# Expert weights in 2 KB rows and quarter-row gathers turned by VectorE, in a one-core transformer block with routed experts

## The chip, the core and the metric

The kernel runs on one core of a Trainium2 chip. A core has a matrix engine (TensorE, called PE in the profile, with its weight loads listed as PEld), a vector engine (VectorE, DVE), a scalar engine (ScalarE, ACT), a general engine (GpSimd, POOL) and a queue engine that only issues transfers (SyncE, SP). All work on a common on-chip memory of 128 partitions, SBUF; TensorE writes its results to a second memory, PSUM. The metric is the time of one execution on the device in microseconds.

## The reference

The block is attention followed by a mixture of experts, on 2048 tokens of 512 features in float32. Only the second half matters here:

```python
h = _layernorm(x) * (1 + cb) + sb
logits = flat @ Wr + router_bias
topk_scores, topk_idx = jax.lax.top_k(softmax(logits), K)      # K = 4 of E = 64 experts
xb = zeros((E, CAP, D)).at[eid, pos].set(flat[tok], mode='drop')   # CAP = 128 seats each
h = silu(einsum('ecd,edh->ech', xb, Wg)) * einsum('ecd,edh->ech', xb, Wu)
yb = einsum('ech,ehd->ecd', h, Wd)
out.at[tok].add(yb[eid, pos] * w)          # plus two shared experts applied to every token
```

Each expert gets up to 128 tokens. Its three matrices are Wg and Wu of 512 x 128 and Wd of 128 x 512.

## The kernel before, in words

Attention runs first, for about 1730 us. Then the output projection is made tile by tile (128 tokens each), normalised, stored to a DRAM array `h2d`, transposed into `h2T`, and routed: `choose`, `positions` and `seat_tokens` build a PSUM table that says which token sits on which seat of which expert. From it the last `seat_tokens` makes `tok` (128 seats x 64 experts of row numbers of `h2d`), lines 998 to 1002.

The expert stage is a software pipeline over 64 experts. For expert e:

- `load_up` (L1088, L1089) and `load_down` (L1094) bring its weights through SP's queue, three experts ahead. Feature k*128+p lies in partition p, block k, so every row of the transfer is 512 bytes.
- `load_xb` (L1323) lets POOL gather the expert's 128 token rows of 2 KB from `h2d` by `tok`, one indirect transfer per expert, three buffers deep.
- `expert_turn` (L1333, L1335) transposes the gathered tile on TensorE, four 128 x 128 blocks into the PSUM tile `tpx`, which ScalarE copies to `xbT`.
- `expert_up` (L1340) multiplies the four blocks of `xbT` by the weights into the PSUM tile `pse`, of which there is only one (`bufs=1`). ScalarE and VectorE make `he` of it (L1099 to L1101).
- `expert_mid` (L1355, L1357) transposes `he`, and `expert_down` (L1361, L1363) multiplies by Wd into `psy`, scales it to `y` and lets ACT's queue store it to `ybd`.

`expert_step(e)` puts four pieces in this order: the turn of expert e+1, with the gather of e+3 ahead of it; the up product of e; the middle of e-1; the down product of e-2. Each piece has a cost in columns: 512, 1024, 128 and 512.

A second stream, the shared experts, is merged with the first. Its units are products into the PSUM tiles `pst` (L1195, three buffers, read by VectorE at L1207 to L1235), and its down products are blocks of 16 matmul records, `psd` (L1257). `merge` takes the piece of whichever stream has done the smaller share of its total cost, and so fixes the program order on each engine. There is no other scheduler: each engine works through its own instructions in that order, and waits where a semaphore tells it to. After the stage a tail gathers the expert outputs from `ybd` and adds them up.

Just ahead of the stage lies the head, ten shared products (`LEAD`) with the last routing steps between them; the last `seat_tokens` comes after product 7, and `token_sum` and `weight_sum` follow on VectorE.

Of the kernel before, what the change touches and what calls it, by code (L numbers as in the profile page):

```python
# [18 lines left out]
P = 128  # L19
# [4 lines left out]
def adaln_block_kernel(  # L24
# [43 lines left out]
    ident = const.tile([P, P], F32)  # L68
# [11 lines left out]
    h2d = dram.tile([N, D], F32)  # L80
# [40 lines left out]
    with ExitStack() as att:  # L121
# [140 lines left out]
        with tc.tile_pool(name="pre", bufs=1) as pre, tc.manual_schedule():  # L262
# [401 lines left out]
        xts = {}  # L664
# [138 lines left out]
    keep = ctx.enter_context(tc.tile_pool(name="keep", bufs=1))  # L803
# [8 lines left out]
    psO = ctx.enter_context(tc.tile_pool(name="psO", bufs=2, space=PSUM))  # L812
# [5 lines left out]
    rt = rts.enter_context(tc.tile_pool(name="rt", bufs=1))  # L818
# [4 lines left out]
    iota = rt.tile([P, E], F32)  # L823
    places = rt.tile([P, CAP], F32)
    own = rt.tile([P, 1], F32)
    tok = keep.tile([CAP, E], U32)
    hs_ = {}
    mvs = {}
    logits = {}
# [5 lines left out]
    def route_consts():  # L835
        nc.sync.dma_start(out=wr, in_=Wr.rearrange("(k p) e -> p k e", p=P))
        nc.sync.dma_start(out=rb, in_=router_bias.partition_broadcast(P))
        make_upper_triangular(nc, before, val=1.0, diag=False)
        nc.gpsimd.memset(onesb, 1.0)
        nc.gpsimd.iota(  # L840
            iota, pattern=[[1, E]], base=0, channel_multiplier=0,
            allow_small_or_imprecise_dtypes=True,
        )
        nc.gpsimd.iota(
            places, pattern=[[1, CAP]], base=0, channel_multiplier=0,
            allow_small_or_imprecise_dtypes=True,
        )
        nc.gpsimd.iota(
            own, pattern=[[0, 1]], base=0, channel_multiplier=1,
            allow_small_or_imprecise_dtypes=True,  # L850
        )

    def load_x(j):
        nc.sync.dma_start(
            out=acc[:, 4 * j : 4 * j + 4, :],
            in_=x[0, j * 512 : (j + 1) * 512, :].rearrange("(i p) d -> p i d", p=P),
        )
# [125 lines left out]
    def seat_tokens(b):  # L983


        t0, nt = BLOCKS[b]
        seat, who = seats.pop(b)
        for n in range(nt * K):
            i, k = divmod(n, K)
            nc.tensor.matmul(  # L990
                out=table,
                lhsT=seat[:, n, :],
                rhs=who[:, i, k].rearrange("p j e -> p (j e)"),
                start=(b == 0 and n == 0),
                stop=(b == len(BLOCKS) - 1 and n == nt * K - 1),
            )
        if b == len(BLOCKS) - 1:
            tb = rt.tile([CAP, 2 * E], F32, name="tb")
            nc.vector.tensor_copy(tb, table)
            nc.vector.scalar_tensor_tensor(  # L1000
                tok, tb[:, E:], float(P), tb[:, :E], ALU.mult, ALU.add
            )

    table = psO.tile([CAP, 2 * E], F32, name="table", tag="tr")
    ALL = ((0, 4), (4, 8), (8, 12), (12, 16))
# [12 lines left out]
    with tc.manual_schedule():  # L1018
# [18 lines left out]
        for t in range(NE, NT):  # L1037
            pr, i = divmod(t, 2)
            if i == 0 and 3 <= pr < NP - 1:
                load_ab(pr + 1, heads=ALL)  # L1040
            if i == 1 and pr >= NP - 1 - S:
                s = pr - (NP - 1 - S)
# [31 lines left out]
    with ExitStack() as ex:  # L1074
# [9 lines left out]
        downs = {}  # L1084

        def load_up(e):
            w = ewp.tile([P, DC, 2, HE], F32, name="wgu")
            nc.sync.dma_start(out=w[:, :, 0, :], in_=Wg[e].rearrange("(k p) h -> p k h", p=P))  # L1088
            nc.sync.dma_start(out=w[:, :, 1, :], in_=Wu[e].rearrange("(k p) h -> p k h", p=P))  # L1089
            weights[e] = w  # L1090

        def load_down(e):
            downs[e] = ewp.tile([P, D], F32, name="wd")
            nc.sync.dma_start(out=downs[e], in_=Wd[e])  # L1094

        def glu(dst, pg, pu, width):

            sig = sgp.tile([P, width], F32, name=f"sig{width}")
            nc.scalar.activation(sig, pg, AF.Sigmoid)  # L1099
            nc.vector.tensor_mul(sig, sig, pg)  # L1100
            nc.vector.tensor_mul(dst, sig, pu)  # L1101
# [213 lines left out]
        xbp = wts.enter_context(tc.tile_pool(name="xbp", bufs=2))  # L1315
        xbs = {}
        xts = {}
        ups = {}
        hts = {}

        def load_xb(e):
            xbs[e] = xbp.tile([CAP, D], F32, name="xb", bufs=3)
            nc.gpsimd.indirect_dma_start(  # L1323
                out=xbs[e][:, :],
                out_offset=None,
                in_=h2d[:, :],
                in_offset=bass.IndirectOffsetOnAxis(ap=tok[:, e : e + 1], axis=0),
            )

        def expert_turn(e):  # L1330
            tp = psO.tile([P, DC, P], F32, name="tpx", tag="tr")
            for k in range(DC):
                nc.tensor.transpose(tp[:, k, :], xbs[e][:, k * P : (k + 1) * P], ident)  # L1333
            xts[e] = xbp.tile([P, DC, CAP], F32, name="xbT")
            nc.scalar.copy(xts[e], tp)  # L1335

        def expert_up(e):
            ps = psO.tile([P, 2 * HE], F32, name="pse", tag="pl", bufs=1)
            for k in range(DC):
                nc.tensor.matmul(  # L1340
                    out=ps,
                    lhsT=xts[e][:, k, :],
                    rhs=weights[e][:, k].rearrange("p i h -> p (i h)"),
                    start=(k == 0),
                    stop=(k == DC - 1),
                )
            if e + 3 < E:
                load_up(e + 3)
            he = xbp.tile([CAP, HE], F32, name="he")
            glu(he, ps[:, :HE], ps[:, HE:], HE)  # L1350
            ups[e] = he

        def expert_mid(e):
            tp = psO.tile([P, CAP], F32, name="tph", tag="tr")
            nc.tensor.transpose(tp, ups[e], ident)  # L1355
            hts[e] = xbp.tile([P, CAP], F32, name="heT")
            nc.scalar.copy(hts[e], tp)  # L1357

        def expert_down(e):
            ps = psO.tile([CAP, D], F32, name="psy", tag="y")  # L1360
            nc.tensor.matmul(out=ps, lhsT=hts[e], rhs=downs[e], start=True, stop=True)  # L1361
            y = xbp.tile([CAP, D], F32, name="y")
            nc.vector.tensor_mul(y, ps, gb)  # L1363
            nc.scalar.dma_start(out=ybd[e * CAP : (e + 1) * CAP, :], in_=y)

        def expert_step(e):
            out = []

            def turn():
                if e + 3 < E:  # L1370
                    load_xb(e + 3)
                expert_turn(e + 1)

            def down():
                expert_down(e - 2)
                if e + 1 < E:
                    load_down(e + 1)

            if e + 1 < E:
                out.append((512, turn))  # L1380
            if e < E:
                out.append((1024, lambda: expert_up(e)))
            if 0 <= e - 1 < E:
                out.append((128, lambda: expert_mid(e - 1)))
            if e >= 2:
                out.append((512, down))
            return out
# [20 lines left out]
                store(t)  # L1408

        with tc.manual_schedule():  # L1410
            for e in range(3):
                load_xb(e)
            expert_turn(0)
            for j in range(1, 5):
                weight_sum(0, j)
            experts = []
            for e in range(E + 2):
                experts += expert_step(e)
            merge([experts, shared[LEAD:-TAIL]], [])
        wts.close()  # L1420
        ygp = ex.enter_context(tc.tile_pool(name="ygp", bufs=4, side="right"))
        with tc.manual_schedule():
# [55 lines left out]
```

## Time and profile before

| What | us |
|---|---|
| Median of three runs (2456.49 to 2463.15) | 2459.82 |
| The profiled execution's own time | 2473.66 |
| Its span in the profile | 2471.9 |
| PE busy in the span | 2376.8 |
| DVE busy | 1512.2 |
| ACT busy | 838.1 |
| POOL busy | 224.1 |
| Expert stage, from the first up product to the last (1974 to 2335) | 361 |

The page names every group of instructions by line, engine and tile, for example `L1340 PE MATMUL pse<-wgu,xbT`: line 1340, TensorE, the result `pse` out of `wgu` and `xbT`. Behind it stand the shapes, the count, the busy time in us, the mean duration of one in ns, and the idle time ahead of it with what ended it. A float32 product shows as two records for each matmul of the program, a transpose as one. The ends of matmuls are modelled: the distance between the starts of two neighbours is what the engine takes for one. A timeline row gives a start and a duration in us.

### The profile page before, as it was taken

Reading aid. Unit: us, or ns where it says so; the run is one execution under the profiler, and the core shown is the slowest. Engines: PE = TensorE matmul, PEld = TensorE weight load, DVE = VectorE, ACT = ScalarE, POOL = GpSimd, SP = SyncE. Lnnn points to the kernel's source line nnn. Section 1 sums busy time; section 2 is a strip of 40 time slices with the busy share of each in tenths; the row PEclk is TensorE's granted clock in tenths of the full one; section 3 lists DMA queues with packets and bytes.
Section 4 is the critical chain, followed back from the end, with each engine's and each line's share of the span. In section 5 each row is a group of like instructions: output and inputs, shape, how many; then the busy total and the mean of one; then the engine's idle time right before and its main releaser. Section 6 shows DMA issues by size and latency. Waiting matters only on the chain. (4 is left out here: it accounts for less than half of the span.)

```text
span 2471.9 us, 26333 instructions
## 1 busy us (share of the span) xinstructions
PE 2376.8 (96%) x8406; PEld 1504.6 (61%) x8406; DVE 1512.2 (61%) x2878; ACT 838.1 (34%) x1785; POOL 224.1 (9%) x286
## 2 busy tenths in 40 slices
PE   7999999999999999999999999998999999999989
PEld 3656656566565665666656656555444476877734
DVE  5367666676666766667667676663655563644654
ACT  3244443443444434444344444432111222222200
POOL 0000000000000000000000000000000011111163
PEclk9999999999999999999999999999999999999989
DMA  4234444454354443444445444564432378778564
GB/s 137 62 79 113 116 118 106 97 135 107 94 133 104 101 119 91 111 111 104 116 96 122 105 103 118 161 174 128 152 119 85 102 206 249 230 212 252 171 190 133
DMA packets 223682, 325.23 MB, mean 132 GB/s; under 512 B 31876, under 2 KB 138424, under 8 KB 223544
## 3 DMA queue, kind: packets, MB, share of 16 engines
q1 hardware_dynamic: 196664, 252.21, 39.5%
q0 software_dynamic: 17664, 54.54, 7.3%
q10 hardware_dynamic: 9216, 16.78, 1.8%
q8 instruction: 68, 1.11, 0.2%
q14 instruction: 70, 0.57, 0.1%
HBM read 138.86 MB, written 41.94 MB: 73 GB/s over the span
## 5 line engine op out<-in xcount | busy, mean ns | idle before, releaser
L516 ACT ACTIVATE p<-ps,nm 128x1024 f32<-128x1024 f32 (+7 forms) x384 | 332.2, 865 | 897.0 <-DVE nm L514 411.5
L569 PE MATMUL po<-pt,v 128*128 128x256 f32 (+1 forms) x2304 | 575.5, 369 | 38.4 <-ACT at L578 33.4
L569 PEld LDWEIGHTS po<-pt,v 128*128 128x128 f32 x2304 | 426.5, 191 | 288.2 <-issue 190.5
L497 PE MATMUL ps<-kt,qt 128*128 128x512 f32 (+3 forms) x1280 | 531.2, 531 | 19.2 <-ACT p L516 16.8
L510 DVE TENSOR_REDUCE nm<-ps 128x1 f32<-128x1024 f32 (+7 forms) x384 | 348.8, 908 | 56.6 <-PE ps L497 47.8
L551 DVE STREAM_TRANSPOSE pt<-pt 128x1664 f32<-128x1664 f32 (+2 forms) x160 | 317.9, 1987 | 44.1 <-DMA pt<-p 40.5
L497 PEld LDWEIGHTS ps<-kt,qt 128*128 128x128 f32 x1280 | 234.7, 190 | 179.2 <-issue 137.0
L424 PE MATMUL pv<-wv,hT 128*128 128x256 f32 x1024 | 240.8, 379 | 2.2 <-ACT v L431 2.2
L581 POOL DMA_DIRECT2D atd<-at x128 | 80.1, 627 | 1649.4 <-ACT at L578 1111.7
L424 PEld LDWEIGHTS pv<-wv,hT 128*128 128x128 f32 x1024 | 194.4, 190 | 31.2 <-ACT v L431 3.0
L704 ACT ACTIVATE p<-p,rs 128x1024 f32<-128x1024 f32 (+7 forms) x256 | 200.0, 805 | 6.2 <-DVE rs L472 5.8
L509 DVE TENSOR_TENSOR ps<-ps,causal 128x128 f32<-128x128 f32 x256 | 74.1, 289 | 176.9 <-PE ps L497 174.5
L1048 PE MATMUL pso<-hT,T 128*128 128x512 f32 x384 | 175.6, 602 | 0.0
L217 PE MATMUL pqk<-T,sw 128*128 128x512 f32 x360 | 169.2, 592 | 0.0
L1340 PE MATMUL pse<-wgu,xbT 128*128 128x256 f32 x512 | 121.1, 379 | 0.0
L1048 PEld LDWEIGHTS pso<-hT,T 128*128 128x128 f32 x384 | 70.3, 193 | 72.1 <-issue 71.3
L217 PE MATMUL pqk<-hT,wq 128*128 128x512 f32 x240 | 113.7, 596 | 0.0
L1257 PE MATMUL psd<-wsd,hs 128*128 128x512 f32 x256 | 111.5, 592 | 0.0
L1340 PEld LDWEIGHTS pse<-wgu,xbT 128*128 128x128 f32 x512 | 93.8, 190 | 11.7 <-issue 1.0
L217 PEld LDWEIGHTS pqk<-T,sw 128*128 128x128 f32 x360 | 68.4, 190 | 47.7 <-issue 43.0
L1323 POOL DMA_INDIRECT xb<-h2d,tok x64 | 65.1, 1018 | 302.2 <-PE tpx L1333 273.0
L1335 ACT COPY xbT<-tpx 128x512 f32<-128x512 f32 x64 | 37.4, 586 | 145.7 <-DVE y L1363 58.0
(364 smaller groups left out, 2364.9 us busy)
## 6 DMA issues: line engine op xcount, KB each, us to landing
pt<-p SPq DMA_DIRECT2D x768, 104.0 KB
pt<-p SPq DMA_DIRECT2D x256, 124.0 KB
pt<-p SPq DMA_DIRECT2D x256, 108.0 KB
atd<-at POOLq DMA_DIRECT2D x128, 128.0 KB
wgu<-in_L_ffn_Wg_dram SPq DMA_DIRECT2D x64, 256.0 KB
wgu<-in_L_ffn_Wu_dram SPq DMA_DIRECT2D x64, 256.0 KB
wd<-in_L_ffn_Wd_dram SPq DMA_DIRECT2D x64, 256.0 KB
ybd<-y ACTq DMA_DIRECT2D x64, 256.0 KB
```

The source lines that it names most:

```text
L217: nc.tensor.matmul(out=ps, lhsT=l[:, k], rhs=r[:, k], start=(k == 0), stop=(k == 1))
L424: nc.tensor.matmul(out=ps, lhsT=hTs[t // 4][:, k, (t % 4) * P : (t % 4 + 1) * P], rhs=wv[:, k].rearrange("p i d -> p (i d)"), start=(k == ...
L497: nc.tensor.matmul(out=ps[:, o : o + wo], lhsT=q, rhs=kts[hd, (c0 + o) // 512][:, :wo], start=True, stop=True,)
L510: nc.vector.tensor_reduce(nm[:, n : n + 1], ps[:, :w], AX.X, ALU.max, negate=True)
L516: nc.scalar.activation(rows[:, r0 + c0 // P : r0 + (c0 + w) // P], ps[:, :w].rearrange("q (r b k) -> q r b k", b=4, k=32), AF.Exp, bias=nm ...
L551: nc.vector.transpose(part, part)
L569: nc.tensor.matmul(out=po if wide else po[:, P:], lhsT=vts[g, kt // 4][:, kt % 4, hh * DH : (hh + 1) * DH], rhs=rows[:, r : r + last + 1 : ...
L581: nc.gpsimd.dma_start(out=atd[hd, :, pr * 256 : (pr + 1) * 256], in_=at)
L704: nc.scalar.activation(part, part, AF.Identity, scale=r)
L1048: nc.tensor.matmul(out=ps, lhsT=abs_[pr][:, hd, i * P : (i + 1) * P], rhs=wos[hd // 4][:, hd % 4, :], start=(hd == 0), stop=(hd == H - 1),)
L1257: nc.tensor.matmul(out=ps, lhsT=hsh[b, f][:, i * P : (i + 1) * P], rhs=wsd[:, f, :], start=(f == 0), stop=(f == NHC - 1),)
L1340: nc.tensor.matmul(out=ps, lhsT=xts[e][:, k, :], rhs=weights[e][:, k].rearrange("p i h -> p (i h)"), start=(k == 0), stop=(k == DC - 1),)
```

## The change

The features of the expert stage are laid out anew: four neighbouring features share a partition (feature 4p+k instead of k*128+p). A partition's part of Wg or Wu is then one run of 2 KB. The turned tokens must have the same layout, and this comes about in two ways:

- `whole(e)`, for the first six experts and for each fourth after them (20 of 64): gathered as before, and transposed on TensorE with every fourth column of the gathered tile as the stationary operand.
- The other 44: four gathers of 128 quarter rows (512 bytes) put quarter a of each token into partitions 32a to 32a+31, and one VectorE instruction transposes 32 x 32 blocks from `xb` straight to `xbT`. TensorE, PSUM and ScalarE take no part.

The quarter gathers need their own row numbers, `tokq`, made once: `pick` (a rearranged identity, built by POOL) and four small products into PSUM (`psq`), then one VectorE instruction. The gathered tiles have four buffers instead of three, and the gather runs four experts ahead. A turn on VectorE counts as 0 in the merge.

```diff
+    quarter = rt.tile([P, 1], F32)
+    pick = rt.tile([P, 4, 4, 32], F32)
     tok = keep.tile([CAP, E], U32)
+    tokq = keep.tile([P, 4, E], U32)
...
+        for b in range(4):
+            nc.gpsimd.memset(quarter[32 * b : 32 * (b + 1), :], float(b))
+            nc.gpsimd.tensor_copy(pick[:, :, b, :], ident.rearrange("p (t r) -> p t r", r=32))
...
             nc.vector.scalar_tensor_tensor(
-                tok, tb[:, E:], float(P), tb[:, :E], ALU.mult, ALU.add
+                tb[:, :E], tb[:, E:], float(P), tb[:, :E], ALU.mult, ALU.add
             )
+            nc.vector.tensor_copy(tok, tb[:, :E])
+            ps = psO.tile([P, 4, E], F32, name="psq", tag="tr")
+            for b in range(4):
+                nc.tensor.matmul(out=ps[:, b, :], lhsT=pick[:, b].rearrange("p a r -> p (a r)"),
+                                 rhs=tb[:, :E], start=True, stop=True)
+            nc.vector.tensor_scalar(tokq, ps, 4.0, quarter, ALU.mult, ALU.add)
...
-            w = ewp.tile([P, DC, 2, HE], F32, name="wgu")
-            nc.sync.dma_start(out=w[:, :, 0, :], in_=Wg[e].rearrange("(k p) h -> p k h", p=P))
-            nc.sync.dma_start(out=w[:, :, 1, :], in_=Wu[e].rearrange("(k p) h -> p k h", p=P))
+            w = ewp.tile([P, 2, DC, HE], F32, name="wgu")
+            nc.sync.dma_start(out=w[:, 0], in_=Wg[e].rearrange("(p k) h -> p k h", k=DC))
+            nc.sync.dma_start(out=w[:, 1], in_=Wu[e].rearrange("(p k) h -> p k h", k=DC))
...
+        def whole(e):
+            return e < 6 or e % 4 == 0
         def load_xb(e):
-            xbs[e] = xbp.tile([CAP, D], F32, name="xb", bufs=3)
...
+            else:
+                xbs[e] = xbp.tile([P, D], F32, name="xb", bufs=4)
+                for b in range(4):
+                    nc.gpsimd.indirect_dma_start(
+                        out=xbs[e][:, b * P : (b + 1) * P],
+                        out_offset=None,
+                        in_=h2d.rearrange("n (b f) -> (n b) f", b=4),
+                        in_offset=bass.IndirectOffsetOnAxis(ap=tokq[:, b, e : e + 1], axis=0),
+                    )
         def expert_turn(e):
...
-                nc.tensor.transpose(tp[:, k, :], xbs[e][:, k * P : (k + 1) * P], ident)
+                nc.tensor.transpose(tp[:, k, :], xbs[e].rearrange("s (p k) -> s k p", k=DC)[:, k, :], ident)
...
+            else:
+                xt = xbp.tile([P, DC, CAP], F32, name="xbT")
+                nc.vector.transpose(
+                    xt.rearrange("p k (b s) -> p b k s", s=32),
+                    xbs[e].rearrange("p (b r k) -> p b k r", b=4, k=DC),
+                )
...
-                    rhs=weights[e][:, k].rearrange("p i h -> p (i h)"),
+                    rhs=weights[e][:, :, k, :],
...
-                if e + 3 < E:
-                    load_xb(e + 3)
+                if e + 4 < E:
+                    load_xb(e + 4)
...
-                out.append((512, turn))
+                out.append((512 if whole(e + 1) else 0, turn))
```

More of the change, by code (lines that the diff above doesn't have):

```diff
@@ L1000, in seat_tokens @@
             nc.vector.scalar_tensor_tensor(
-                tok, tb[:, E:], float(P), tb[:, :E], ALU.mult, ALU.add
+                tb[:, :E], tb[:, E:], float(P), tb[:, :E], ALU.mult, ALU.add
             )
+            nc.vector.tensor_copy(tok, tb[:, :E])
+            ps = psO.tile([P, 4, E], F32, name="psq", tag="tr")
+            for b in range(4):
+                nc.tensor.matmul(
+                    out=ps[:, b, :],
+                    lhsT=pick[:, b].rearrange("p a r -> p (a r)"),
+                    rhs=tb[:, :E],
+                    start=True,
+                    stop=True,
+                )
+            nc.vector.tensor_scalar(tokq, ps, 4.0, quarter, ALU.mult, ALU.add)
     table = psO.tile([CAP, 2 * E], F32, name="table", tag="tr")
@@ L1319, in adaln_block_kernel @@
         hts = {}
+        def whole(e):
+            return e < 6 or e % 4 == 0
         def load_xb(e):
-            xbs[e] = xbp.tile([CAP, D], F32, name="xb", bufs=3)
[L1323 to L1328, printed above, removed]
-        def expert_turn(e):
[L1331 to L1335, printed above, removed]
+            if whole(e):
+                xbs[e] = xbp.tile([CAP, D], F32, name="xb", bufs=4)
+                nc.gpsimd.indirect_dma_start(
+                    out=xbs[e][:, :],
+                    out_offset=None,
+                    in_=h2d[:, :],
+                    in_offset=bass.IndirectOffsetOnAxis(ap=tok[:, e : e + 1], axis=0),
+                )
+            else:
+                xbs[e] = xbp.tile([P, D], F32, name="xb", bufs=4)
+                for b in range(4):
+                    nc.gpsimd.indirect_dma_start(
+                        out=xbs[e][:, b * P : (b + 1) * P],
+                        out_offset=None,
+                        in_=h2d.rearrange("n (b f) -> (n b) f", b=4),
+                        in_offset=bass.IndirectOffsetOnAxis(ap=tokq[:, b, e : e + 1], axis=0),
+                    )
+        def expert_turn(e):
+            if whole(e):
+                tp = psO.tile([P, DC, P], F32, name="tpx", tag="tr")
+                for k in range(DC):
+                    nc.tensor.transpose(tp[:, k, :], xbs[e].rearrange("s (p k) -> s k p", k=DC)[:, k, :], ident)
+                xt = xbp.tile([P, DC, CAP], F32, name="xbT")
+                nc.scalar.copy(xt, tp)
+                xts[e] = [xt[:, k, :] for k in range(DC)]
+            else:
+                xt = xbp.tile([P, DC, CAP], F32, name="xbT")
+                nc.vector.transpose(
+                    xt.rearrange("p k (b s) -> p b k s", s=32),
+                    xbs[e].rearrange("p (b r k) -> p b k r", b=4, k=DC),
+                )
+                xts[e] = [xt[:, k, :] for k in range(DC)]
         def expert_up(e):
@@ L1341, in expert_up @@
                     out=ps,
-                    lhsT=xts[e][:, k, :],
-                    rhs=weights[e][:, k].rearrange("p i h -> p (i h)"),
+                    lhsT=xts[e][k],
+                    rhs=weights[e][:, :, k, :],
                     start=(k == 0),
@@ L1410, in adaln_block_kernel @@
         with tc.manual_schedule():
-            for e in range(3):
+            for e in range(4):
                 load_xb(e)
```

## The prediction

> **What bounds the kernel now.** I read the busy table first, then the stretches of the expert stage, then its groups by shape, and last the timeline of two neighbouring experts.
>
> ```profile
> PE 2376.8 (96%) x8406; PEld 1504.6 (61%) x8406; DVE 1512.2 (61%) x2878; ACT 838.1 (34%) x1785; POOL 224.1 (9%) x286
> ```
>
> ```profile
> 2104.00:2195.00 91.00, 91.00 (x431) 73.60 (x430) 58.57 (x142) 23.12 (x61) 17.62 (x16) 1.00 0.78 231
> 2195.00:2255.00 60.00, 60.00 (x220) 36.27 (x219) 15.93 (x36) 10.85 (x32) 9.47 (x10) 1.00 0.71 207
> 1974.00:2335.00 361.00, 361.00 (x1576) 268.13 (x1575) 186.98 (x446) 82.29 (x224) 61.04 (x60) 1.00 0.75 222
> ```
>
> The stretches give busy time of PE, PEld, DVE, ACT and POOL, then the granted clock, the DMA share and GB/s. From the first up product to the last, TensorE has no idle time, at full clock. VectorE is busy for 64% of the first stretch shown (shared units between the experts) and 27% of the second (down blocks between them). In the list of waits over this stage no TensorE row waits for a transfer.
>
> ```profile
> L1333 PE MATMUL tpx<-ident,xb 128*128 128x128 f32 x256 | 38.3, 273 | 0.0
> L1335 ACT COPY xbT<-tpx 128x512 f32<-128x512 f32 x64 | 37.4, 586 | 145.7 <-DVE y L1363 58.0 <-PE tpx L1333 37.3 <-PE pse L1340 21.9
> L1323 POOL DMA_INDIRECT xb<-h2d,tok x64 | 65.1, 1018 | 302.2 <-PE tpx L1333 273.0 <-issue 26.7 <-DMA xb<-h2d,tok 2.5
> ```
>
> These are the three groups that the change touches per expert. POOL's 302 us of idle time show that it waits for tiles to be free, not the reverse.
>
> ```profile
> 2035.22 0.27 PE L1355 MATMUL tph<-ident,he 128*128 128x128 f32 x1
> 2035.33 1.02 PE L1361 MATMUL psy<-wd,heT 128*128 128x512 f32 x2
> ...
> 2035.42 0.28 ACT L1099 ACTIVATE sig<-pse 128x128 f32<-128x128 f32 x1 [1.09 <-PE pse L1340]
> ...
> 2036.05 0.29 DVE L1101 TENSOR_TENSOR he<-sig,pse 128x128 f32<-128x128 f32 x1
> 2036.19 0.60 PE L1333 MATMUL tpx<-ident,xb 128*128 128x128 f32 x4
> ...
> 2036.62 1.89 PE L1340 MATMUL pse<-wgu,xbT 128*128 128x256 f32 x8
> ```
>
> Here two experts follow each other with no shared work between. The distance from `tpx` to `pse`, 2036.62 - 2036.19 = 0.43 us, is what TensorE pays for one turn. And `pse` has one buffer: the next product cannot start before `he` has been read out of it, at 2036.05 + 0.29 = 2036.34. There are 0.28 us to spare.
>
> **The change part by part.** *Turns taken off TensorE.* 44 experts x 0.43 us = 18.9 us, on the engine that sets the end: -18.9. ScalarE also loses 44 copies of 0.586 us; it was 23% busy, so nothing is gained by that.
>
> *What stops part of the gain.* In the program order of the changed kernel 13 of 63 neighbouring pairs of up products have no shared work between them, 9 of them without a turn on TensorE. There TensorE would arrive at 2036.19 on the clock of the rows above, but `he` ends at 2036.34. The time from a VectorE end to the product that waits for it lies between 0 and the 0.28 us seen; I take the middle, 0.15. Such a pair gains 0.13 us, not 0.43: 9 x 0.30 = +2.7. In the other pairs the timeline shows 1.04 us or more between the end of `he` and the next up product.
>
> *The transpose on VectorE.* The large transposes of attention (L551) take 1906 ns for 1664 columns and 2241 ns for 1984: 1.047 ns a column and 164 ns fixed, so 0.70 us for 512. This read goes in steps of 16 bytes, which L551 does not. The Trainium skill speaks against that (SBUF — State Buffer, in the section Door 1: The DMA port swizzle): memory lines hold 16 bytes, and an access that opens a new line pays unless at least two hits fall on each. In float32 each element here opens one. The trace has two strided rows:
>
> ```profile
> L923 DVE TENSOR_REDUCE mask<-oh x8: 1036/1041/1046, 1763.5 to 1955.3; 128x128 bf16<-128x512 bf16 x8
> L928 DVE TENSOR_REDUCE taken<-mask x7: 286/286/290, 1764.5 to 1921.7; 128x64 bf16<-128x128 bf16 x7
> ```
>
> Both step over 128 bytes. L923 needs 1041 ns where the dense reduction of 512 elements (L957) needs 686; L928 needs 286 ns, no more than the dense L903 over as many elements. So the penalty is between none and (1041 - 164) / (686 - 164) = 1.7 times, that is 0.70 to 1.06 us. Either way 44 of them add 31 to 47 us to 187 us of VectorE work in 361 us, 60 to 65%, and it stays under TensorE. What it can delay are the three `pst` buffers: in the timeline the release of one lies at least 0.65 us ahead of the matmul that writes it again, with eight cases under 2.2 us. A transpose queued ahead of such a read, with TensorE 0.43 us sooner, uses up a few of these: 0 to 4 us, I take +1.5. The `he` pairs above bear 1.04 us of spare time against 0.43 + 0.70, and VectorE is mostly idle when they come, so nothing more.
>
> *The 20 turns that stay on TensorE* now load every fourth column as weights. No row shows a strided weight load. If it costs nothing, a turn stays at 0.43 us; if each of four loads of 0.107 us (a quarter of 0.43) opens four times as many lines and takes four times as long, the turn takes 1.72 us and 20 of them +25.8. With L923's 1.7 times the turn would take 0.73 us, +6.0; with L928's none, 0. VectorE reading SBUF is the nearest row to another engine reading SBUF, so I take the middle of these two: +3.0, and keep 0 and 25.8 as ends. By the page alone, which names no factor, it would be a loss of unknown size; by the rows, 0 to 6.
>
> *The quarter gathers.* Each of the 44 issues three gathers more: 132 x 1.018 us, with 0.30 us between neighbours (first two gathers: 1967.03 for 1.08 us, then 1968.41). Per four experts POOL works 13 x 1.32 = 17.1 us, while TensorE takes (361 - 18.9) / 64 x 4 = 21.4 us. It is covered, with 80% of the cover used; per gather the limit is 21.4 / 13 = 1.65 us. Queued behind a gather that waits are only further gathers; what they feed is the transpose, and a late one would hold VectorE. Before, a gather had two steps until its turn, and no turn waited; now it has three, a step of 3.1 to 5.9 us more, against 3 x 1.32 = 4.0 us until the last quarter is issued. Hence 0. The same page (A bandwidth-pool intuition that's wrong) says that a VectorE operation in a two-port mode blocks POOL's descriptor writing entirely. No row tells whether a transpose is one; the present gathers, beside a busy VectorE, run from 943 to 1445 ns. I use the mean; with the longest throughout, (1.445 + 0.30) x 13 = 22.7 us, POOL would be just too slow.
>
> *2 KB weight rows.* No TensorE row waits for `wgu`, so faster landing is worth 0; the cover is the three experts of lead. The bytes stay the same, and SP's issue (0.37 and 0.50 us a pair) is one queue's own time.
>
> *`tokq`.* The four `psq` products stand in TensorE's order right behind the seats. These end at about 1965.1 (where the next product starts); VectorE can finish `tb` only at 1965.79 + 0.23 = 1966.02. So TensorE waits 0.9 us plus a handover of 0.15. The products: L889's eight records of 128 x 64 take 0.83 us (1931.10 to 1931.93), and these are eight such records. Together +1.9. VectorE meanwhile waits for `psq` and then makes `tokq`, about 1.5 us; behind it are two token sums and four weight sums, first needed at 1973.79, five microseconds after they ended (1968.68). The first gather starts about 1.6 us later, as TensorE does. POOL's `pick` and `quarter` fall into its 3.28 us of idle time ahead of the first store of `h`; eight instructions of the size of its iotas (0.13 to 0.23 us) fit: 0.
>
> *Sum.* -18.9 + 2.7 + 1.5 + 3.0 + 1.9 = -9.8 us. The profiled execution took 2473.66 us, 1.8 us more than its span; 2463.9 of 2473.66 is 0.9960, and of the median 2459.82 this is 2450.
>
> **The rivals.** *Nearly nothing remains* (2456). The freed TensorE time turns into waits for `he` and `pst`: if VectorE's transposes come at 1.06 us and each of 29 experts between shared units loses 0.2 us, that is 6 us more: -4. For it: 64% busy VectorE in those stretches, in bursts. Against it: spare times of 1 to 3 us.
>
> *Slower, by the strided weight loads* (2472). At four times per load: -18.9 + 2.7 + 1.5 + 25.8 + 1.9 = +13. It decides from 0.64 us more per turn, a load 2.5 times as long as now. For it the 16-byte lines; against it that nothing in the trace is above 1.7.
>
> *Slower, by POOL* (2469, if every gather takes the longest time seen, 1.445 us, and 0.30 between): 22.7 against 21.4 us per four experts, over 14.5 fours 19 us; with the sum's -9.8 that is 9 us slower than before. It decides from 1.65 us.
>
> *The full gain* (2443): strides free, no new waits: -18.9 + 1.9 = -17.
>
> **How the numbers follow.** Case by case: the sum, 0.48; the full gain, 0.10; nearly nothing, 0.22; strided loads, 0.14; POOL, 0.06. A measurement of this kernel cannot tell less than 0.3% (7.4 us) from no change. Faster by more than that: 0.58; within: 0.22; slower: 0.20. The likeliest case alone runs from 2444 to 2454; to hold eight of ten the range takes in the full gain and the near half of the slower cases: 2441 to 2470.
>
> **What would show it.** `tpx` groups down to 80 records, their start-to-start distance 0.11 us if strides are free, towards 0.18 or 0.4 if not. A transpose row of 44 at 0.70 to 1.06 us. TensorE waits on `he` in nine pairs, below 0.2 us each. POOL's gathers 196 at about 1.0 us, with its idle time still ended by freed tiles. One wait of a microsecond at `psq`. I am wrong if VectorE's transposes wait for a gather, if the stage is not 8 to 14 us shorter than 361, or if the attention part moves.

## The result, and the profile after

The changed kernel took 2446.18 us (median of 6 runs, 2439.05 to 2448.79) beside 2458.34 us for the kernel before: a ratio of 0.9944, 95% interval 0.9927 to 0.9961. The prediction had said 2450 of 2459.82, 0.9960. Measured twice more beside its variants, the ratio was 0.9929 (0.9911 to 0.9946) and 0.9967 (0.9954 to 0.9980). In one set of experiments, the first, the kernel before itself took 2472.62 us, 14 to 16 us more than in all others, and variants with quarter gathers took up to 83 us more than they did later, so these variants are judged by their later runs.

Whole runs of one kernel differ by up to 12 us, and the profiled run of the kernel before has a tail (after its last up product) of 140.7 us where the changed one has 126.3 for the same work. That profiled run took 2473.66 us, about as long as the kernel before took in the first set. In its tail TensorE stands still for 8.6 us between 2384 and 2400 us, and from 2330 us on the mean granted clock (the share of TensorE's full speed that it was given) is 0.95, where the changed kernel has a single gap of 0.63 us and 1.00. In the stage itself both ran at 1.00, and the kernel before without a gap. So most readings below are of the expert stage alone, from the start of the first `pse` row to the start of the last. That length repeats: 339.17, 339.16 and 339.16 us in three profiles of the changed kernel. In the kernel before it is 2329.33 - 1974.65 = 354.68 us, read from one profile. (The 361 us given ahead of the prediction run to 2335, 3.8 us past the end of the last up product.) Line numbers have moved: `pse` is L1384, `tpx` L1369, `tph` and `psy` L1399 and L1405, `he` L1120.

The first and last up product in the timeline of TensorE, in the kernel before:

```profile
1974.65 1.89 PE L1340 MATMUL pse<-wgu,xbT 128*128 128x256 f32 x8
...
2329.33 1.89 PE L1340 MATMUL pse<-wgu,xbT 128*128 128x256 f32 x8
```

and in the changed kernel:

```profile
1972.68 1.89 PE L1384 MATMUL pse<-wgu,xbT 128*128 128x256 f32 x8
...
2311.85 1.89 PE L1384 MATMUL pse<-wgu,xbT 128*128 128x256 f32 x8
```

The stage is 15.5 us shorter. The busy table of its page, and then the same stretches as in the prediction (PE, PEld, DVE, ACT, POOL, then clock, DMA share and GB/s):

```profile
PE 2352.3 (96%) x8238; PEld 1486.0 (61%) x8238; DVE 1555.5 (64%) x2924; ACT 815.2 (33%) x1741; POOL 350.8 (14%) x426
```

```profile
2104.00:2195.00 91.00, 90.91 (x388) 70.00 (x387) 67.91 (x149) 17.08 (x51) 51.74 (x54) 1.00 0.75 237
2195.00:2255.00 60.00, 59.53 (x215) 37.90 (x214) 29.97 (x59) 7.65 (x27) 35.97 (x39) 1.00 0.78 254
1972.00:2315.00 343.00, 341.98 (x1391) 250.41 (x1391) 227.12 (x485) 58.09 (x179) 185.06 (x191) 1.00 0.74 233
```

TensorE is still full: it has lost work, and gained 1.0 us of recorded idle time. VectorE has gone from 187 to 227 us of the stage and POOL from 61 to 185, and beyond the pairs shown below little of that reaches TensorE's time. The groups by shape that the change touched:

```profile
L1358 POOL DMA_INDIRECT xb<-h2d,tokq x176 | 170.6, 969 | 131.1 <-issue 43.6 <-DVE xbT L1375 40.7 <-DVE sig L1119 35.3
L1375 DVE STREAM_TRANSPOSE xbT<-xb 128x512 f32<-128x512 f32 x44 | 48.3, 1098 | 0.0
L1349 POOL DMA_INDIRECT xb<-h2d,tok x20 | 19.6, 981 | 34.0 <-DVE tokq L1020 27.4 <-issue 4.3 <-PE tpx L1369 1.1
L1369 PE MATMUL tpx<-ident,xb 128*128 128x128 f32 x80 | 12.6, 282 | 0.0
L1371 ACT COPY xbT<-tpx 128x512 f32<-128x512 f32 x20 | 11.6, 586 | 41.0 <-PE tpx L1369 15.7 <-PE pst L1214 12.7 <-DVE y L1407 9.1
```

`tpx` is down to 80 records, and the transpose on VectorE takes 1098 ns and is never preceded by idle time: it never waited for its gathers. POOL still has idle time to spare, 40.7 of 131.1 us of it ended by a transpose that frees a tile.

Where the stage's time went is read most exactly from TensorE's timeline by adding up, for each tile, the time from the start of its row to the start of the next row on the engine. The table does this between the first and the last up product (the last included) for the kernel before, the changed kernel, and three kernels of the experiments. `tph`, 6.8 us in each of them, is left out. The row `pst` shows what late reads by VectorE would cost.

| us to the next row, by tile | before | all whole | changed | 58 quarter | 58 quarter, two banks |
|---|---|---|---|---|---|
| `tpx`, turns | 27.08 | 29.24 | 8.49 | 1.89 | 1.90 |
| `psy`, down products | 52.50 | 52.50 | 54.97 | 55.96 | 52.46 |
| `pse`, up products | 110.59 | 110.62 | 111.20 | 111.57 | 110.56 |
| `pst`, shared units | 104.51 | 104.53 | 104.52 | 104.49 | 104.43 |
| `psd`, shared down | 54.95 | 54.96 | 54.93 | 54.95 | 54.92 |
| first to last `pse` start | 354.68 | 356.90 | 339.17 | 333.91 | 329.37 |

Of the changed kernel, `tpx` gives 18.6 us, and `psy` and `pse` take 3.1 us back. Those are the pairs of experts with no shared work between them, in the timeline:

```profile
2043.98 0.27 PE L1399 MATMUL tph<-ident,he 128*128 128x128 f32 x1
2044.09 1.02 PE L1405 MATMUL psy<-wd,heT 128*128 128x512 f32 x2
...
2044.82 0.29 DVE L1120 TENSOR_TENSOR he<-sig,pse 128x128 f32<-128x128 f32 x1
...
2045.20 1.97 PE L1384 MATMUL pse<-wgu,xbT 128*128 128x256 f32 x8
2047.01 0.27 PE L1399 MATMUL tph<-ident,he 128*128 128x128 f32 x1
```

From `psy` to the next row it is 0.86 us elsewhere; here it is 1.11, and `pse` starts 0.09 us after `he` has been read out. Seven such pairs show 1.11 us and two 1.22; nine pairs, as predicted. What the further 0.11 us of these two are isn't shown; there `pse` starts 0.21 us after `he` ends.

Ahead of the stage, the seats and the product behind them in the kernel before:

```profile
1964.67 0.61 PE L990 MATMUL table<-who,seat 128*128 128x128 bf16 x8
1965.11 3.65 PE L1111 MATMUL psg<-h2T,wsg 128*128 128x512 f32 x8
```

and in the changed kernel, with the four products for `tokq` between them:

```profile
1960.66 0.61 PE L997 MATMUL table<-who,seat 128*128 128x128 bf16 x8
...
1961.79 0.23 DVE L1007 SCALAR_TENSOR_TENSOR tb<-tb 128x64 f32<-128x64 f32 x1
...
1962.16 1.08 PE L1013 MATMUL psq<-tb,pick 128*128 128x64 f32 x8 [0.89 <-DVE tb L1007]
1963.07 3.22 PE L1130 MATMUL psg<-h2T,wsg 128*128 128x512 f32 x7
```

From the seats to the next `psg` it is 1963.07 - 1960.66 = 2.41 us, where the kernel before takes 1965.11 - 1964.67 = 0.44. That is 1.97 us of TensorE's time given back.

### The profile page after: what moved, and what is told of

Same layout as the page of the kernel before. It is cut to its first block, busy times and chain, and to the rows that moved or that the text cites. A ratio compares the mean times of both kernels' runs of the same rounds, so it can differ in the third digit from the quotient of the medians.

```text
span 2440.0 us, 26185 instructions
## 1 busy us (share of the span) xinstructions
PE 2352.3 (96%) x8238; PEld 1486.0 (61%) x8238; DVE 1555.5 (64%) x2924; ACT 815.2 (33%) x1741; POOL 350.8 (14%) x426
## 3 DMA queue, kind: packets, MB, share of 16 engines
q8 instruction: 66, 1.08, 0.2%
## 5 line engine op out<-in xcount | busy, mean ns | idle before, releaser
L569 PE MATMUL po<-pt,v 128*128 128x256 f32 (+1 forms) x2304 | 574.8, 369 | 37.6 <-ACT at L578 32.4
L551 DVE STREAM_TRANSPOSE pt<-pt 128x1664 f32<-128x1664 f32 (+2 forms) x160 | 317.9, 1987 | 44.2 <-DMA pt<-p 40.7
L1358 POOL DMA_INDIRECT xb<-h2d,tokq x176 | 170.6, 969 | 131.1 <-issue 43.6
L1384 PE MATMUL pse<-wgu,xbT 128*128 128x256 f32 x512 | 121.6, 380 | 1.0 <-PE psy L1405 0.4
L1384 PEld LDWEIGHTS pse<-wgu,xbT 128*128 128x128 f32 x512 | 95.9, 190 | 30.3 <-issue 7.4
L484 DVE TENSOR_SCALAR p<-p,rs 128x1024 f32<-128x1024 f32 (+3 forms) x128 | 84.2, 700 | 2.3
```

Of the source, the lines that this page charges most:

```text
L551: nc.vector.transpose(part, part)
L569: nc.tensor.matmul(out=po if wide else po[:, P:], lhsT=vts[g, kt // 4][:, kt % 4, hh * DH : (hh + 1) * DH], rhs=rows[:, r : r + last + 1 : ...
L1358: nc.gpsimd.indirect_dma_start(out=xbs[e][:, b * P : (b + 1) * P], out_offset=None, in_=h2d.rearrange("n (b f) -> (n b) f", b=4), in_offse ...
L1384: nc.tensor.matmul(out=ps, lhsT=xts[e][k], rhs=weights[e][:, :, k, :], start=(k == 0), stop=(k == DC - 1),)
```

## The experiments

The theory: TensorE sets the stage's end, so each of the 44 turns taken off it is worth what a turn costs there, less the wait for `he` in nine pairs; the wider rows of the weights bring nothing. The rivals: the rows bring part of it; VectorE's slower transposes or POOL's gathers hold a part back.

Four variants were run first, then the changed kernel again with two variants, then the changed kernel with three of the first four once more, then one last kernel. Whole times are compared within a set only; the length of the stage, which repeats, is compared across the later sets too. The variants with other numbers of turns also change the program order, as a turn on VectorE counts as 0 in the merge; the table has no time for an effect of the order by itself, as `pst` and `psd` agree within 0.1 us in all five kernels.

### All experts whole

```diff
         def whole(e):
-            return e < 6 or e % 4 == 0
+            return True
```

> The changed kernel with all 64 experts gathered whole and turned on TensorE; the 2 KB weight rows, the strided turns, tokq and the four buffers stay. My theory: the gain is the 44 turns taken off TensorE, nothing else. Then this is as slow as the kernel before or a little slower: 64 turns at 0.47 instead of 0.435 us are +2 us, the wait and products of psq +2 us, so 2460 to 2464 us, the stage from first to last up product about 357 us. Rival, the 2 KB weight rows bring the gain: it stays at about 2446 us, the stage at about 340 us.

Measured in the first set: 2475.12 us, ratio 1.0011 (1.0001 to 1.0020). Once more later:

> All 64 experts whole, the new rows and the products with tb kept. Theory (the gain is the 44 turns): 2460 to 2464 beside a kernel before of 2458, that is 17 to 21 us above the changed kernel: 44 x 0.47 = 20.7 for the turns. Rival (the 2 KB rows bring part of the gain): under 2456.

Measured: 2463.78 us beside 2456.96, ratio 1.0029 (1.0015 to 1.0044), in the range of the theory. Above the changed kernel of the same set it is 15.0 us in whole runs, less than the 17 to 21 named, and 17.7 us in the stage. The stage took 356.90 us in both sets. Nothing of the gain is left without the turns: the kernel is 2.2 us slower in the stage than the one before. Weight loads of `tpx` in the kernel before, by shape:

```profile
L1333 PEld LDWEIGHTS tpx<-ident,xb 128*128 128x128 f32 x256 | 31.9, 141 | 26.8 <-issue 21.7 <-ACT sig L1099 3.6
```

and in this one, with the products that they serve:

```profile
L1369 PEld LDWEIGHTS tpx<-ident,xb 128*128 128x128 f32 x256 | 40.6, 204 | 23.3 <-issue 19.0 <-ACT sig L1118 3.6
L1369 PE MATMUL tpx<-ident,xb 128*128 128x128 f32 x256 | 40.5, 282 | 0.0
```

A load of every fourth column takes 204 ns instead of 141, 1.45 times. But loads overlap the products, and a turn of four costs TensorE only 29.24 / 62 = 0.472 us instead of 27.08 / 62 = 0.437 (62 of the 64 turns lie in the stage). That 0.035 us x 62 = 2.2 us is all of the difference in the stage.

The wider rows show in the queue list as fewer packets and little else. Packets, MB, and the share of 16 engines' time on the weights' queue, in the kernel before:

```profile
q1 hardware_dynamic: 196664, 252.21, 39.5%
```

and in the changed kernel:

```profile
q1 hardware_dynamic: 147512, 252.21, 39.4%
```

With the spans of the two profiles that is 976 and 961 us of the 16 engines' time, so the same bytes take 1.5% less. The Trainium skill (DMA: Bandwidth & Descriptors, section Specifications) puts the smallest transfer for line rate at 512 B, the row that the kernel before already had; these figures agree with it.

### The changed kernel again, and every second expert

> The changed kernel itself once more, beside its variants. Theory A (the stalls of the variants belong to quarter gathers on this chip and not to the edits): it stalls as they do, 2485 to 2500 us where the kernel before takes 2472, a ratio of 1.005 to 1.010. Theory B (they come from the edits): ratio 0.993 to 0.996 again, 2455 to 2462 us beside 2472 or 2442 to 2450 beside 2458, and TensorE is busy in over 49.5 of every 50 us of the expert stage.

Measured: 2440.53 us (2437.44 to 2443.65) beside 2458.33, ratio 0.9929 (0.9911 to 0.9946); stage 339.16 us. That is theory B, with the time and the ratio just under the ranges named.

```diff
         def whole(e):
-            return e < 6 or e % 4 == 0
+            return e < 6 or e % 2 == 0
```

> From expert 6 on every second expert in quarter rows, 29 in place of 44: 35 whole turns on TensorE instead of 20. Theory A (quarter gathers stall this chip): it lies between the kernel before and the changed kernel here, about two thirds of the way. Theory B (each turn off TensorE is worth 0.43 us and nothing else acts): 15 x 0.47 = 7 us slower than the changed kernel, 29 x 0.43 less the 4 us of waits and products = 8 us faster than the kernel before; POOL's load of 8 quarter and 2 whole gathers per four experts is 13 us of 21, so it is never late.

Measured: 2450.42 us, ratio 0.9969 (0.9956 to 0.9983), with the changed kernel at 2440.53 and the kernel before at 2458.33 in the same set. The stage is 346.18 us: 7.0 us more than in the changed kernel, for 15 turns at 0.47 us, as expected; in whole runs it is 9.9 us. In its timeline seven pairs show 1.22 us behind `psy`.

### Two halves of one bank for the up product

```diff
-            ps = psO.tile([P, 2 * HE], F32, name="pse", tag="pl", bufs=1)
+            if not pse2:
+                pse2.append(psO.tile([P, 2, 2 * HE], F32, name="pse", tag="pl", bufs=1))
+            ps = pse2[0][:, e % 2]
```

> The changed kernel with the up products alternating between the two halves of one PSUM bank, so that one need not wait until he has been read out of it. Theory: nine pairs of experts without a TensorE turn and without shared work between them lose 0.2 to 0.3 us each to this wait; it goes, -2 to -3 us (2443 to 2444), and the shortest distances between the end of he and the next up product, 0.09 to 0.21 us now, become negative. Rival: the waits move on to the next thing (heT, psy, the transpose) and the time stays at 2446.

Measured in the first set: 2496.43 us, ratio 1.0092 (1.0070 to 1.0113).

> The up products in two halves of one PSUM bank by turns, the rest as changed, beside the changed kernel on the same chip. If the compact pairs' wait costs what the prediction charged (nine pairs, 2.7 us), it lies 2 to 3 us below the changed kernel on this chip, whatever that takes here. If writing a product into a bank while the other half is read costs something, it lies above it, by 20 to 50 us if the stalls seen with it earlier are its own.

Measured: 2447.39 us beside 2440.53 for the changed kernel, ratio to the kernel before 0.9954 (0.9935 to 0.9972), which overlaps with that of the changed kernel. In whole runs that is 6.9 us above the changed kernel, within the spread of both, where 2 to 3 below were expected. The stage is 338.82 us: 0.34 us gained. The same kind of pair in its timeline:

```profile
2048.40 1.02 PE L1408 MATMUL psy<-wd,heT 128*128 128x512 f32 x2
2049.12 0.29 DVE L1120 TENSOR_TENSOR he<-sig,pse 128x128 f32<-128x128 f32 x1
2049.46 0.73 PEld L1387 LDWEIGHTS pse<-wgu,xbT 128*128 128x128 f32 x4 [0.87 <-DVE he L1120]
```

The product goes to the other half, and still waits for `he`. The edit didn't take the wait away, so the run says nothing of what the wait costs. The Trainium skill (PSUM — Partial Sum Buffer, section PSUM bank collisions raise a hardware error) says that accesses of different engines have to be kept apart by bank, not by address. The row can't test that: the two halves are also one tile of the program, so it doesn't show whether the wait goes by the bank or by the tile, and no run here shows what the chip would do without it. The last experiment uses another tile in another bank.

### Most experts in quarter rows

```diff
         def whole(e):
-            return e < 6 or e % 4 == 0
+            return e < 6
```

> The changed kernel with only the first six experts whole, 58 in quarter rows. Theory, TensorE is still what sets the pace and POOL has room: 14 more turns of 0.47 us go, less some waits, 2440 to 2444 us; POOL's gathers 58 x 4 + 6 = 238, about 5.1 us of each expert's 5.2. Rival, POOL is the bound as soon as all experts take four gathers: transposes wait for gathers, VectorE stands still, 2447 to 2460 us.

Measured in the first set: 2523.33 us, ratio 1.0202 (1.0185 to 1.0219). Later, first the changed kernel as the yardstick of the set:

> The changed kernel, as the yardstick of this call. If what disturbed the first set of variants belongs to a time and not to the kernels, then here either the kernel before takes 2458 and this one 2440 to 2446 (undisturbed), or the kernel before takes 2472 and this one 2485 to 2500 (disturbed, and quarter gathers suffer most).

Measured, the changed kernel: 2448.79 us beside 2456.96, ratio 0.9967 (0.9954 to 0.9980), stage 339.16 us: as in the other sets in the stage, with the whole run at the long end of its spread and above the 2446 named. Then the 58:

> From expert 6 on all in quarter rows, 58 of them. Without a POOL limit 14 more turns off TensorE give 14 x 0.47 = 6.6 us below the changed kernel, 2434. POOL has 16 gathers x 1.25 = 20.0 us per four experts, against the 19.5 us of TensorE that are left per four bare experts. Theory (POOL becomes the bound): it is at or above the changed kernel, 2441 to 2470. The first set of runs gave 1.020 to the kernel before; if that was the disturbed time and not POOL, it is 2434 here.

Measured: 2440.09 us, ratio 0.9932 (0.9919 to 0.9945), below the changed kernel of the same set, and the stage is 333.91 us, 5.3 us shorter. So the theory in that text, POOL as the bound, was wrong. POOL issues a gather each 0.97 + 0.30 = 1.27 us; 16 of them are 20.3 us, and four experts take 333.91 / 63 x 4 = 21.2 (the stage from first to last `pse` is 63 steps). With 96% of the cover used it still holds nobody up: the list of waits has no VectorE row that waits for a gather. The 14 turns gave 6.6 us (`tpx`, 8.49 to 1.89), and 14 pairs now wait for `he` instead of nine: 1.4 us back in `psy` and `pse`.

### Dense reads in the transpose

VectorE's transpose reads 32 neighbouring elements instead of every fourth. The features of `xb` then no longer stand against their own rows of the weights: this kernel computes other products of the same size.

```diff
-                    xbs[e].rearrange("p (b r k) -> p b k r", b=4, k=DC),
+                    xbs[e].rearrange("p (b k r) -> p b k r", b=4, k=DC),
```

> The changed kernel with the VectorE transpose reading 32 neighbouring elements instead of every fourth; the features then do not match those of the weights, so the expert outputs are other numbers, but every instruction, size and wait stays. Theory: the 16-byte step is what makes the transpose 1.10 us long; dense it takes 0.70 us, as the attention transposes scale to, and since VectorE is not the bound the time moves by 0 to -3 us (2443 to 2446). Rival: VectorE's lateness costs TensorE time in the shared units; then 44 x 0.40 us less work there gives 5 to 10 us (2436 to 2441).

Measured in the first set: 2490.35 us, ratio 1.0067 (1.0051 to 1.0083).

> VectorE's transposes read 32 neighbouring elements in place of every fourth (features of xb then do not answer to the rows of the weights, so the output is that of other products): 0.70 us each in place of 1.10. If VectorE's time sets the end, 44 x 0.40 = up to 17.6 us below the changed kernel; if VectorE is covered by TensorE, as the prediction had it, the same within 3 us. The first set of runs gave 1.0067 to the kernel before; if that was a disturbed time, it is 0.992 to 0.995 here.

Measured: 2441.88 us, ratio 0.9941 (0.9928 to 0.9954). Its transposes, by shape:

```profile
L1375 DVE STREAM_TRANSPOSE xbT<-xb 128x512 f32<-128x512 f32 x44 | 30.9, 702 | 0.0
```

Each is 0.40 us shorter, 17.4 us in all, and the stage is 339.16 us, the same as in the changed kernel to 0.01 us. VectorE's time is hidden completely. The step of 16 bytes costs 1098 / 702 = 1.56 times.

### A second bank for the up product

On the kernel with 58 in quarter rows, so compared with that one:

```diff
-            ps = psO.tile([P, 2 * HE], F32, name="pse", tag="pl", bufs=1)
+            if e % 2:
+                ps = psO.tile([P, 2 * HE], F32, name="pse", tag="gu", bufs=3)
+            else:
+                ps = psO.tile([P, 2 * HE], F32, name="pse", tag="pl", bufs=1)
```

> All in quarter rows from expert 6 on, and the up product of every odd expert goes to one of the three banks of the shared products, so that neighbouring products have different banks. Beside the kernel with 58 in quarter rows and one bank (expert stage 335.8 us, TensorE 55.96 us behind the down products and 111.57 behind the up products, where the kernel with none in quarter rows has 52.50 and 110.62). Theory (the wait for he in the compact pairs costs 0.35 us a pair): these two go back to 52.5 to 53 and 110.6 to 110.8, the stage to 331.5 to 333, if the shared products, with two banks left at times, do not wait in turn; then the run takes some 3 to 4 us less than with one bank, a ratio of 0.990 to 0.993 to the kernel before. Rival (what ends last behind he is VectorE's transpose or the weights, right behind it): under 1 us is gained. If the shared products want their third bank, pst rises above 104.6 and the stage is 336 or longer.

Measured: 2434.39 us (2431.30 to 2442.22) beside 2457.73, ratio 0.9910 (0.9889 to 0.9931). The stage is 329.37 us, 4.5 us shorter than with one bank. (The 335.8 us in the text above run to the end of the last up product, 1.89 us more; so counted it is 331.26 us here, just under the 331.5 to 333 named.) A pair in the timeline with one bank:

```profile
2047.22 1.02 PE L1405 MATMUL psy<-wd,heT 128*128 128x512 f32 x2
2047.95 0.29 DVE L1120 TENSOR_TENSOR he<-sig,pse 128x128 f32<-128x128 f32 x1
2048.33 1.97 PE L1384 MATMUL pse<-wgu,xbT 128*128 128x256 f32 x8
```

and one with two:

```profile
2049.03 1.02 PE L1408 MATMUL psy<-wd,heT 128*128 128x512 f32 x2
2049.75 0.29 DVE L1120 TENSOR_TENSOR he<-sig,pse 128x128 f32<-128x128 f32 x1
2049.89 1.89 PE L1387 MATMUL pse<-wgu,xbT 128*128 128x256 f32 x8
```

`psy` to `pse` falls from 1.11 to 0.86 us, and `pse` starts before `he` ends. In the table `psy` and `pse` fall back to what they are with no turn on VectorE at all (52.46 and 110.56), and `pst` doesn't rise (104.43): the shared products don't miss their third bank. So 14 pairs cost 4.5 us, 0.32 each, shown by taking the wait away. Whether the other bank or only the other tile did it isn't separated. This kernel has the shortest stage here, 9.8 us shorter than the changed one's. In whole runs the interval of its ratio still overlaps with that of the kernel with one bank (0.9919 to 0.9945) and with two of the changed kernel's three (0.9927 to 0.9961 and 0.9911 to 0.9946).

### What the first set had

The kernel with 58 in quarter rows took 401.59 us for its stage in the first set and 333.91 later; the dense reads 369.50 and 339.16; the two halves 374.54 and 338.82. With all experts whole it was 356.90 in both. So in the stage whatever was at work met only the kernels with quarter gathers. In the timeline of the first set's kernel with 58, a block of 16 shared down products and VectorE's addition that reads it:

```profile
2059.57 7.03 PE L1276 MATMUL psd<-wsd,hs 128*128 128x512 f32 x16
...
2070.44 0.69 DVE L1283 TENSOR_TENSOR acc<-acc,psd 128x512 f32<-128x512 f32 x1 [9.75 <-PE tph L1399]
```

and later:

```profile
2053.16 7.03 PE L1276 MATMUL psd<-wsd,hs 128*128 128x512 f32 x16
...
2060.22 0.69 DVE L1283 TENSOR_TENSOR acc<-acc,psd 128x512 f32<-128x512 f32 x1 [5.95 <-PE psd L1276]
```

VectorE sat idle for 9.75 us and got the block 10.87 us after its recorded start, where 7.06 is usual, while TensorE's records run on without a gap up to 2069.4. Over the whole stage they do have gaps. The stretch of the stage in the first set:

```profile
1978.00:2381.00 403.00, 355.73 (x1324) 250.76 (x1323) 236.18 (x493) 48.59 (x164) 225.86 (x233) 0.95 0.62 198
```

and later:

```profile
1972.00:2315.00 343.00, 341.79 (x1358) 246.68 (x1357) 241.62 (x504) 51.08 (x168) 227.81 (x236) 1.00 0.74 235
```

TensorE has 47.3 us without recorded work instead of 1.2, and the granted clock is 0.95 instead of 1.00: it falls to half in ten stretches, 37.6 us in all, and each begins within 4 us after a gap begins. Estimated from these figures, the gaps give 46 us and the clock 19, together 65 of the 68 us. The dense reads and the two halves show the same on a smaller scale (idle 20 and 24 us more, clock 0.98). The durations of POOL's gathers are the same in both sets (969 and 970 ns). So what the lost time consists of is clear; what opened the gaps, and why in the stage only with quarter gathers, the runs don't settle. The changed kernel itself wasn't run in that set; the dense reads, with as many gathers, were slower there than the kernel before.

## Why the prediction was right

Step by step, in us of TensorE's time, the prediction's term against what the table and the rows show:

| Step | predicted | measured |
|---|---|---|
| 44 turns off TensorE | -18.9 | -19.2 (44 x 0.437) |
| Strided loads in the turns that stay | +3.0 (0 to 25.8) | +0.6 (18 of them in the stage x 0.035) |
| Nine pairs that wait for `he` | +2.7 | +3.1 (`psy` +2.47, `pse` +0.61) |
| VectorE late in freeing `pst` | +1.5 (0 to 4) | 0.0 (`pst` 104.51 to 104.52) |
| `psq` ahead of the stage | +1.9 | +2.0 |
| Sum | -9.8 | -13.5 |

- *The turns.* Right, and shown to be the gain's only source by the kernel with all experts whole, and to scale by the number of turns with 29, 44 and 58.
- *The pairs.* Right in place, number and size. The extra beside 0.27 us behind `psy` is some 0.07 in the product itself: after such a wait it takes 1.81 us to the next row (2045.20 to 2047.01) instead of 1.73. The time from the end of `he` to `pse` is 0.09 us where 0.15 was taken.
- *The strided weight loads.* The step that was mis-sized. The rows of VectorE (none to 1.7 times) did carry over to the load, 1.45 times; the mistake was to let the longer load lengthen the whole turn by the same factor. Four loads are 4 x 0.063 = 0.25 us longer by their records, and the turn 0.035 us: the rest doesn't show, as the loads run beside the products. The rival at 2472, which needed 0.64 us more per turn, falls by a factor of 18.
- *The transposes.* 1098 ns, above the predicted 0.70 to 1.06; the size didn't matter, since 0.40 us less of each moved the stage by 0.01 us. Dense it took the 0.70 us that the prediction had worked out, so the penalty that it took from the rule of the 16-byte lines is there, 1.56 times, and VectorE had the room for it.
- *`pst`.* No release came late enough to cost anything, although VectorE has 227 us of work in 343. The 1.5 us were the other term that was too large.
- *POOL.* 1.27 us a gather against the limit of 1.65; the kernel with 58 shows that even 96% of the cover is enough. The gathers beside the transposes took 941 to 1442 ns, 969 in the mean, where they took 943 to 1445 before. So no blocking of POOL by the transposes shows, the danger that the prediction had left open.
- *The rows of 2 KB.* 0, as predicted.
- *The rivals.* By the sum of the steps, the change came out midway between the likeliest case (-9.8) and the full gain (-17), and by whole runs at -12.2, -17.8 and -8.2 in the three sets. That the first of these lies so near the forecast is in part luck, as the sets differ by more than the two terms that were too large, 3.9 us together. What bears out the account is the stage, term by term. Nearly nothing remaining, and slower by POOL, both rested on waits for VectorE or POOL of which the table shows nothing.
- *The signs named in advance.* The stage is 15.5 us shorter, just outside the 8 to 14 named, since 3.9 us of the feared costs did not come (the 361 of that sign is the longer count; the stage between the marks was 354.68). In the nine pairs the product starts 0.09 us (seven) and 0.21 us (two) after `he` ends, but TensorE's waits are 0.25 and 0.36 us: "below 0.2" did not agree with the 0.30 a pair of the sum itself. And the part ahead of the stage is not steady enough to be read: the first up product starts at 1972.68, 1972.96 and 1971.46 us in three profiles of the changed kernel, 1974.65 in the one before, although 2.0 us were added there.

The sum of -13.5 against the median of 2458.34 would be 2444.8; the changed kernel's 17 runs in three sets have the median 2443.65.

## What to carry to other kernels

When one engine is busy without a gap, moving work off it can pay its full start-to-start price, as it did here, even onto an engine that takes more than twice as long for it, as long as the other engine's time stays covered. What takes part of it back are waits that the removed work used to hide; look in the program order for the places where nothing else stands between a result and the buffer's next write, and give those places a second PSUM bank: here that took the wait away, and a second half of one bank did not. Compare such changes by the length of the stage between two marks on the bounding engine: outside the first set it repeated to 0.01 us here where whole runs spread over 12.

## What was not expected

- A gather by POOL costs the same for 128 rows of 512 bytes as for 128 of 2 KB: 969 and 981 ns, plus 0.30 us between neighbours. So four quarter gathers take POOL four times as long as one whole one.
- A stride of 16 bytes costs TensorE's weight load 1.45 times (141 to 204 ns) and the turn made of four of them 1.08 times (0.437 to 0.472 us).
- The spread of one kernel's runs goes with the mean granted clock: the changed kernel took 2437 to 2439 us in runs with 0.996, 2443 to 2445 with 0.994, and 2447 to 2450 with 0.992 and 0.993. The 0.004 between the ends is 9.8 us of 2440, about what the runs differ by.
- Three kernels with quarter gathers had stages 30 to 68 us longer in the first set than later, and the one without them none. For the two halves, 36 us longer, both runs were on a chip of the same number. The gain of the change was there in each of the three sets in which the changed kernel ran; it is not shown for the condition of the first, where the dense reads, with the same gathers, took 2490.35 us beside 2472.62.
